# Spreading dependent chains over the pairs of a graph-attention kernel, and giving the first loads separate queues

## The chip, the cores and the metric

The kernel runs on one core of a Trainium2 chip. The metric is the time of one execution on the device in microseconds, as the median of several runs. The core has five engines with a queue of instructions each, which they work off in order: TensorE (PE, matmuls and transposes, results in PSUM), VectorE (DVE), ScalarE (ACT), GpSimd (POOL[...]) and SyncE (SP, which here only issues DMAs). DMAs are issued by SP, POOL and, with the change, ScalarE.

## The reference, cut to what matters

Four graph layers run one after the other on x (4096 x 256, float32), with one adjacency matrix adj (4096 x 4096, int32, about 32 neighbours in a row). Layers 0 and 2 hold an additive attention:

```python
h = relu(layernorm(x))
Wh = h @ W                                 # 4096 x 256
e = Wh @ a_src + (Wh @ a_dst).T            # 4096 x 4096
e = where(e > 0, e, slope * e)             # slope 0.2 in layer 0, 0.01 in layer 2
e = where(adj > 0, e, -9e15)               # -1e12 in layer 2
h_attn = softmax(e, axis=1) @ Wh
# layer 0: h_attn goes into a larger dense block, and x = x + block(...)
# layer 2: x = x + elu(h_attn)
```

Layer 1 is a mean over the neighbours, layer 3 an attention with dot products. The change does not touch their own code.

## The kernel before, in words

Rows are taken in tiles of 128 (NT = 32 tiles). The class Attention serves layers 0 and 2. It works in blocks of RB = 4 row tiles (layer 0 begins with two blocks of two), and within a block over the 32 column tiles in 16 pairs (PPB = 16). The loop of `run` has one turn for each pair n. A turn does these things in the source:

- `ahead(n)` (layer 0 only, its call is fresh): adjacency tiles are loaded by POOL's queue (adj_t, L486), transposed on TensorE into cT (L495) and turned by ScalarE into mask codes (turned, L500). FRESH says how many pairs this is ahead. In layer 2 the codes come back from DRAM instead (turned<-codesT on SP, L914).
- `reach(n + PPB + lead)` for a pair of the next block: VectorE keeps a running minimum of code minus destination score in PSUM (run, L278 and L280). LEAD says how many pairs this is ahead.
- `top(b)`, called in the turn in which a block's last minimum is issued: ScalarE copies run into SBUF (run_sb, L291), TensorE transposes it (top, L294), VectorE reduces and makes two rows of offsets from it (m and ab, L297 to L302), TensorE transposes these (abT, L304), ScalarE copies abT (L306), and it goes out to DRAM and back to all partitions as ab_row (SP, L319 and L320). Blocks 0 to 2 of layer 0 spread it by matmuls instead (L313, `spread` is 3).
- `logits` of pair n: VectorE makes y from ab_row and a PSUM copy b of it (L332; ScalarE makes b once a block, L330), and POOL subtracts the code (L336). There are eight buffers of y.
- Three pairs later (LAG): ScalarE's exponential of y (L363) and TensorE's 16 matmuls into four accumulators acc (L374; eight matmuls in a block of two). Column 0 of v is one, so that column 0 of acc is the sum of the row.
- At a block's last pair: VectorE takes the reciprocal of every sum (rden, L382), and `finish` scales the accumulators, half of them on VectorE and half on ScalarE: `finish0` writes xs (L447, L449), `finish2` writes hp (L926, L930), from which it makes exponential linear units and adds the rows of xs (L934 to L937). Layer 0 has four accumulators, layer 2 five.

PSUM tiles and y are released when their last reader is done. The order of the instructions on each engine is not just that of the source: when the program is built, a scheduler fills each engine's queue from the source's order and its own estimate of when operands are ready. On the chip that order is fixed.

Ahead of layer 0's run stands a preparation (`block0`): eight loads of x (xs, L610, on SP), with W and the two vectors a between the first and the second (L223 and L230, on SP too), then for each of eight blocks statistics, centring (L629, L633), transposes (L145), projections by W (L154) and minima.

## Time and profile before

| | |
|---|---|
| median of 3 runs | 2985.78 us (2985.42 to 2987.26) |
| the profiled execution, its own time | 2990.5 us |
| its span, first to last instruction | 2988.7 us |
| mean granted TensorE clock | 0.989 |
| TensorE busy (matmuls) | 2866.0 us |
| VectorE, ScalarE, POOL busy | 1907.1, 1279.1, 947.8 us |
| layer 0, preparation and attention | 0 to 626 us |
| layer 0, dense part | 626 to 1240 us |
| layer 1 | 1240 to 1500 us |
| layer 2, attention | 1531 to 2016 us |
| layer 3 | 2016 to 2989 us |

The profile comes from one execution. A group's line names the source line, the engine, the operation, the output and inputs by the program's names, shapes and count, then the busy time and the mean of one in ns, then the idle time of that engine just before these instructions and what ended it. In a list of waits a line reads "engine, waiting instruction <- engine, instruction it waited for: us in total, times, longest". A timeline's line has the start, the duration, the instruction, its count, and in brackets the idle time before it with what ended it.

### The profile page before, as it was taken

Reading aid. Unit: us, or ns where it says so; the run is one execution under the profiler, and the core shown is the slowest. Engines: PE = TensorE matmul, PEld = TensorE weight load, DVE = VectorE, ACT = ScalarE, POOL = GpSimd, SP = SyncE. Lnnn points to the kernel's source line nnn. Section 1 sums busy time; section 2 is a strip of 40 time slices with the busy share of each in tenths; the row PEclk is TensorE's granted clock in tenths of the full one; section 3 lists DMA queues with packets and bytes.
Section 4 is the critical chain, followed back from the end, with each engine's and each line's share of the span. In section 5 each row is a group of like instructions: output and inputs, shape, how many; then the busy total and the mean of one; then the engine's idle time right before and its main releaser. Section 6 shows DMA issues by size and latency. Waiting matters only on the chain.

```text
span 2988.7 us, 35212 instructions
## 1 busy us (share of the span) xinstructions
PE 2866.0 (96%) x13381; PEld 2335.5 (78%) x13381; DVE 1907.1 (64%) x3458; ACT 1279.1 (43%) x1963; POOL 947.8 (32%) x718
## 2 busy tenths in 40 slices
PE   7989999999999999899989999999999999999999
PEld 5778888866556665788878777888888888888888
DVE  5777777534555554477689888646766566566653
ACT  5666655459997323892264433433212112111211
POOL 4667665544444433220045555540000000000000
PEclk9999999999999999999999999999999999999999
DMA  5766665234553000595342122002111111111100
GB/s 131 201 146 145 128 139 133 71 58 70 80 79 65 8 8 8 136 248 164 113 170 87 68 78 78 29 11 68 58 51 47 37 34 62 39 34 62 34 8 8
DMA packets 109161, 238.62 MB, mean 80 GB/s; under 512 B 10736, under 2 KB 31200, under 8 KB 100288
## 3 DMA queue, kind: packets, MB, share of 16 engines
q1 hardware_dynamic: 71296, 167.26, 16.3%
q0 software_dynamic: 37696, 69.11, 14.9%
q8 instruction: 105, 1.72, 0.2%
q14 instruction: 64, 0.52, 0.1%
HBM read 265.63 MB, written 37.81 MB: 102 GB/s over the span
## 4 chain that ended last, share of the span: by engine, by line
PE 66%; ACT 9%; DVE 8%; issue 6%; POOL 6%; DMA 4%; SPq 0%; POOLq 0%; DVEq 0%; ACTq 0%
PE acc L374 18%; PE acc L1287 15%; PE s L154 15%; PE mm L154 8%; PE acc L1019 8%; POOL y L336 4%; ACT sign L180 4%; DVE y L332 2%; DVE run L280 2%; DMA turned<-codesT 1%; PE cT L495 1%; DMA a<-in_adj_dram 1%; PE q_ps L154 1%; ACT t L712 1%; DMA xs<-in_x_dram 1%
## 5 line engine op out<-in xcount | busy, mean ns | idle before, releaser
L374 PE MATMUL acc<-v,y 128*128 128x257 f32 x4096 | 930.8, 386 | 23.9 <-ACT hp L930 12.7
L374 PEld LDWEIGHTS acc<-v,y 128*128 128x128 f32 x4096 | 776.2, 192 | 137.0 <-ACT hp L930 17.0
L336 POOL TENSOR_TENSOR y<-y,turned 128x1024 f32<-128x1024 f32 (+1 forms) x272 | 545.3, 2015 | 320.2 <-DVE y L332 260.1
L363 ACT ACTIVATE y<-y,sdst 128x512 f32<-128x512 f32 (+1 forms) x544 | 350.5, 690 | 410.9 <-POOL y L336 410.7
L332 DVE SCALAR_TENSOR_TENSOR y<-ab_row,cdst,b 128x512 f32<-128x512 f32 (+1 forms) x544 | 371.0, 710 | 139.9 <-PE acc L374 124.1
L1287 PE MATMUL acc<-v,y 128*128 128x257 f32 x2048 | 454.5, 380 | 0.4 <-DVE rden L1295 0.4
L154 PE MATMUL s<-qT,hT 128*128 128x256 f32 x2048 | 445.2, 379 | 0.7 <-ACT qT L1235 0.7
L1280 ACT ACTIVATE y<-y 128x1024 f32<-128x1024 f32 x128 | 132.2, 1055 | 714.3 <-DVE y L1279 710.0
L154 PEld LDWEIGHTS s<-qT,hT 128*128 128x128 f32 x2048 | 389.0, 190 | 54.2 <-ACT qT L1235 1.4
L1287 PEld LDWEIGHTS acc<-v,y 128*128 128x128 f32 x2048 | 387.1, 190 | 55.9 <-issue 0.8
L180 ACT ACTIVATE sign<-a,limits 128x1024 bf16<-128x1024 bf16 x256 | 293.8, 1148 | 18.5 <-DMA a<-in_adj_dram 13.0
L1249 DVE SCALAR_TENSOR_TENSOR y<-code,s 128x512 f32<-128x512 bf16 x256 | 175.8, 687 | 100.7 <-PE s L154 100.5
L280 DVE SCALAR_TENSOR_TENSOR run<-turned,v,run 128x512 f32<-128x512 bf16 (+1 forms) x279 | 193.2, 692 | 31.8 <-ACT turned L500 22.7
L280 DVE SCALAR_TENSOR_TENSOR run<-turned,dst,run 128x512 f32<-128x512 bf16 x248 | 186.5, 752 | 24.5 <-DMA turned<-codesT 20.4
L1279 DVE TENSOR_TENSOR y<-y,top 128x1024 f32<-128x1024 f32 x128 | 146.2, 1215 | 43.0 <-PE top L1273 43.0
L1256 DVE TENSOR_TENSOR mx<-mx,y 128x512 f32<-128x512 f32 x224 | 154.8, 691 | 7.5
L500 ACT ACTIVATE turned<-cT,log_wide 128x1024 bf16<-128x1024 bf16 x128 | 139.2, 1105 | 29.9 <-PE cT L495 29.5
L173 POOL DMA_DIRECT2D a<-in_adj_dram x128 | 75.1, 588 | 198.4 <-ACT sign L180 144.8
L154 PE MATMUL mm<-kept 128*128 128x512 f32 x288 | 135.5, 610 | 2.4 <-ACT sz L807 1.4
L1019 PE MATMUL acc<-early,eq 128*128 128x512 f32 x512 | 128.8, 401 | 2.2 <-DVE early L421 1.9
L1019 PE MATMUL acc<-late,eq 128*128 128x512 f32 x512 | 122.6, 391 | 0.0
L1019 PEld LDWEIGHTS acc<-early,eq 128*128 128x128 f32 x512 | 97.0, 191 | 26.2 <-DVE early L421 2.1
(233 smaller groups left out, 3007.1 us busy)
## 6 DMA issues: line engine op xcount, KB each, us to landing
turned<-codesT SPq DMA_DIRECT2D x36, 1024.0 KB, 4.8
adj_t<-in_adj_dram POOLq DMA_DIRECT2D x128, 256.0 KB, 5.5
codesT<-turned SPq DMA_DIRECT2D x32, 1024.0 KB, 5.1
a<-in_adj_dram POOLq DMA_DIRECT2D x128, 256.0 KB, 4.7
code<-codesT SPq DMA_DIRECT2D x128, 256.0 KB, 5.5
code<-codesT SPq DMA_DIRECT2D x64, 512.0 KB, 8.1
ab_row<-l_ab_d SPq DMA_DIRECT2D x14, 512.0 KB, 5.6
xs<-in_x_dram SPq DMA_DIRECT2D x8, 512.0 KB, 12.5
```

The source lines that it names most:

```text
L154: nc.tensor.matmul(out=ps, lhsT=lhsT_of(k), rhs=rhs_of(k), start=(k == 0), stop=(k == n - 1))
L180: nc.scalar.activation(sign, self.came[g], AF.Sign, bias=limits[:, v : v + 1], accum_out=over[:, t, v, q : q + 1],)
L280: nc.vector.scalar_tensor_tensor(st["run"], code, dst, st["run"], ALU.subtract, ALU.min)
L332: nc.vector.scalar_tensor_tensor(y[:, :, k, :], st["ab"][:, 0, :, :], self.cdst[:, c + k : c + k + 1], st["b"], ALU.add, ALU.max,)
L336: nc.gpsimd.tensor_tensor(y, y, mask[:, :, c % QT : c % QT + 2, :], ALU.subtract)
L363: nc.scalar.activation(y[:, :, k, :], y[:, :, k, :], AF.Exp, bias=self.sdst[:, c + k : c + k + 1],)
L374: nc.tensor.matmul(out=acc, lhsT=y[:, r, k, :], rhs=self.v[:, c + k, 0 : D + 1], start=(c + k == 0), stop=(c + k == NT - 1),)
L1019: nc.tensor.matmul(out=acc, lhsT=eqs[c // (NT // 2)][:, ts(c % (NT // 2), P)], rhs=v1[c // BT][:, c % BT, :, :], start=(c == 0), stop=(c = ...
L1249: nc.vector.scalar_tensor_tensor(y[:, :, c : c + 2, :], st["code"][:, :, c : c + 2, :], -BIG / UNIT, ps, ALU.mult, ALU.add,)
L1256: nc.vector.tensor_tensor(mx, mx, y[:, :, c : c + 2, :], ALU.max)
L1279: nc.vector.tensor_tensor(part, part, top, ALU.subtract)
L1287: nc.tensor.matmul(out=accs[r], lhsT=st["y"][:, r, c, :], rhs=v3[:, c, :], start=(c == 0), stop=(c == NT - 1),)
```

## The change

What each part does:

- `top` becomes a generator with three pauses. It is put into a list `tasks`, and one link of each task is issued at the end of every turn of `run` (`step`): nothing in the turn of the last minimum, the transposes in the next turn, the reduction in the one after, abT and its way to ab_row in the third. Block 0's is issued at once (`drain`).
- The last minimum of a block writes straight into the SBUF tile run_sb, and ScalarE's copy of run falls away.
- At a block's end ScalarE copies every accumulator's 256 sums (raw) and its column 0 (den) out of PSUM. `finish` is a generator too: one reciprocal of den on VectorE a turn later, then the scaling, in place. In layer 0 VectorE scales. In layer 2 ScalarE scales, POOL takes a minimum, ScalarE the exponential, POOL adds the rows of xs (VectorE does both for the last block), and VectorE ends it, one link a turn.
- W and the two a are issued by ScalarE, so that SP has x alone. Two adjacency tiles instead of one are asked for ahead of the rest.
- LEAD goes from 5 to 6 and FRESH from 8 to 9.

```diff
+        def step(self):
+            for g in list(self.tasks):
+                if next(g, StopIteration) is StopIteration:
+                    self.tasks.remove(g)
+        def drain(self):
+            while self.tasks:
+                self.step()
...
+                to = st["run"]
+                if j == NT - 1:
+                    to = self.row_p.tile([P, RB, P], F32, tag="run", name="run_sb", bufs=1)
+                    to = to[:, 0:n, :]
                 if j == 0:
-                    nc.vector.tensor_scalar(st["run"], code, dst, None, ALU.subtract)
+                    nc.vector.tensor_scalar(to, code, dst, None, ALU.subtract)
                 else:
                     nc.vector.scalar_tensor_tensor(
-                        st["run"], code, dst, st["run"], ALU.subtract, ALU.min
-                    )
+                        to, code, dst, st["run"], ALU.subtract, ALU.min
+                    )
+                st["run"] = to
             if c == NT - 2 and not self.held:
-                self.top(b)
+                self.tasks.append(self.top(b))
+                if b == 0:
+                    self.drain()
         def top(self, b):
-            run = self.row_p.tile([P, RB, P], F32, tag="run", name="run_sb", bufs=1)[:, 0:n, :]
-            nc.scalar.copy(run, st["run"])
+            yield
             ps = self.ps_top.tile([P, RB, P], F32, tag="top", name="top")[:, 0:n, :]
             for r in range(n):
-                nc.tensor.transpose(ps[:, r, :], run[:, r, :], ident)
+                nc.tensor.transpose(ps[:, r, :], st["run"][:, r, :], ident)
+            yield
             src = self.v[:, at : at + n, D + 1]
...
             nc.vector.scalar_tensor_tensor(ab[:, 1, :], src, self.slope, m, ALU.mult, ALU.subtract)
+            yield
             ps = self.ps_top.tile([2 * n, P], F32, tag="top", name="abT")
...
                     if c == NT - 2:
                         done = accs.pop(b)
-                        rden = self.small.tile([P, RB], F32, tag="rden", name="rden")
+                        at, n_r = self.blocks[b]["at"], self.blocks[b]["n"]
+                        den = self.small.tile([P, n_r], F32, tag="den", name="den")
+                        raw = self.room(at, n_r)
                         for r, acc in enumerate(done):
-                            nc.vector.reciprocal(rden[:, r : r + 1], acc[:, 0:1])
-                        self.finish(self.blocks[b]["at"], done, rden)
+                            nc.scalar.copy(raw[:, r, :], acc[:, 1 : D + 1])
+                            nc.scalar.copy(den[:, r : r + 1], acc[:, 0:1])
+                        rden = self.small.tile([P, n_r], F32, tag="rden", name="rden")
+                        self.tasks.append(self.finish(at, raw, den, rden))
+                self.step()
+            self.drain()
...
-    LEAD = 5
+    LEAD = 6
     FIRST = 8
-    FRESH = 8
+    FRESH = 9
...
+            def room0(at, n):
+                return xs[:, at : at + n, :]
+            def finish0(at, raw, den, rden):
+                yield
+                nc.vector.reciprocal(rden, den)
+                for r in range(raw.shape[1]):
+                    nc.vector.tensor_scalar(
+                        raw[:, r, :], raw[:, r, :], rden[:, r : r + 1], None, ALU.mult
+                    )
...
-                load(1)
+                load(2)
+                att.weights(
+                    wp, w["L0_gnn_W"], (w["L0_gnn_a_src"], w["L0_gnn_a_dst"]), nc.scalar
+                )
                 for b in range(NB):
                     nc.sync.dma_start(
                         out=xs[:, ts(b, BT), :],
                         in_=x[ts(b, BW), :].rearrange("(t p) d -> p t d", p=P),
                     )
-                    if b == 0:
-                        att.weights(
-                            wp, w["L0_gnn_W"], (w["L0_gnn_a_src"], w["L0_gnn_a_dst"]), nc.sync
-                        )
...
+    def room2(at, n):
+        return work2.tile([P, RB, D], F32, tag="hp", name="hp")
+    def finish2(at, h, den, rden):
+        last = at == NT - RB
+        yield
+        nc.vector.reciprocal(rden, den)
+        yield
+        for r in range(RB):
+            nc.scalar.activation(
+                h[:, r, :], h[:, r, :], AF.Identity, scale=rden[:, r : r + 1], bias=minus
+            )
+        yield
         e = work2.tile([P, RB, D], F32, tag="e", name="e")
-        nc.scalar.activation(e, h, AF.Exp, bias=ones[:, 0:1])
+        (nc.vector if last else nc.gpsimd).tensor_scalar(e, h, -1.0, None, ALU.min)
+        yield
+        nc.scalar.activation(e, e, AF.Exp, bias=ones[:, 0:1])
+        yield
         rows = xs[:, at : at + RB, :]
-        nc.vector.scalar_tensor_tensor(e, e, 1.0, rows, ALU.min, ALU.add)
+        (nc.vector if last else nc.gpsimd).tensor_tensor(e, e, rows, ALU.add)
+        yield
         nc.vector.scalar_tensor_tensor(rows, h, -1.0, e, ALU.max, ALU.add)
```

More of the change, by code (lines that the diff above doesn't have):

```diff
@@ L192, with __init__ @@
     class Attention:
-        def __init__(self, es, tag, slope, lag, n_y, blocks, turned, finish, ps_top=None):
+        def __init__(self, es, tag, slope, lag, n_y, blocks, turned, room, finish, ps_top=None):
             self.tag, self.slope, self.lag, self.n_y = tag, slope, lag, n_y
-            self.turned, self.finish = turned, finish
+            self.turned, self.room, self.finish = turned, room, finish
+            self.tasks = []
             self.blocks = [{"at": at, "n": n} for at, n in blocks]
@@ L441 @@
         with ExitStack() as es:
-            def finish0(at, accs, rden):
-                for r, acc in enumerate(accs):
-                    dst, by = xs[:, at + r, :], rden[:, r : r + 1]
-                    if r % 2:
-                        nc.vector.tensor_scalar(dst, acc[:, 1 : D + 1], by, None, ALU.mult)
-                    else:
-                        nc.scalar.mul(dst, acc[:, 1 : D + 1], by)
+            def room0(at, n):
[7 more added lines that the diff above has]
+                    )
             turned = {}
@@ L460 @@
             ps_c = es.enter_context(tc.tile_pool(name="ps_c", bufs=2, space=PSUM))
-            att = Attention(es, "l0", 0.2, 3, 8, cuts, turned_of, finish0, ps_c)
+            att = Attention(es, "l0", 0.2, 3, 8, cuts, turned_of, room0, finish0, ps_c)
             att.hold(v0, "right")
@@ L918 @@
     nc.gpsimd.memset(minus, -1.0)
-    def finish2(at, accs, rden):
-        h = work2.tile([P, RB, D], F32, tag="hp", name="hp")
-        for r, acc in enumerate(accs):
-            by = rden[:, r : r + 1]
-            if r % 2:
-                nc.vector.tensor_scalar(
-                    h[:, r, :], acc[:, 1 : D + 1], by, -1.0, ALU.mult, ALU.add
-                )
-            else:
-                nc.scalar.activation(
-                    h[:, r, :], acc[:, 1 : D + 1], AF.Identity, scale=by, bias=minus
-                )
+    def room2(at, n):
[10 more added lines that the diff above has]
+        yield
         e = work2.tile([P, RB, D], F32, tag="e", name="e")
-        nc.scalar.activation(e, h, AF.Exp, bias=ones[:, 0:1])
+        (nc.vector if last else nc.gpsimd).tensor_scalar(e, h, -1.0, None, ALU.min)
+        yield
+        nc.scalar.activation(e, e, AF.Exp, bias=ones[:, 0:1])
+        yield
         rows = xs[:, at : at + RB, :]
-        nc.vector.scalar_tensor_tensor(e, e, 1.0, rows, ALU.min, ALU.add)
+        (nc.vector if last else nc.gpsimd).tensor_tensor(e, e, rows, ALU.add)
+        yield
         nc.vector.scalar_tensor_tensor(rows, h, -1.0, e, ALU.max, ALU.add)
     cuts2 = [(t, RB) for t in range(0, NT, RB)]
-    att2 = Attention(l2, "l2", 0.01, 3, 8, cuts2, None, finish2)
+    att2 = Attention(l2, "l2", 0.01, 3, 8, cuts2, None, room2, finish2)
     one2 = l2.enter_context(tc.tile_pool(name="l2_one", bufs=1))
@@ L1113 @@
                 pass
-            att2.top(0)
+            att2.tasks.append(att2.top(0))
+            att2.drain()
             run_staggered(blocks, 1)
```

## The prediction

> **What bounds the kernel now.** I read the page first, then the chain of waits, then the two attention stages (layer 0 up to 626 us, layer 2 from 1531 to 2016 us) in the timeline of TensorE, because the diff touches only those and the first 60 us.
>
> ```profile
> PE 2866.0 (96%) x13381; PEld 2335.5 (78%) x13381; DVE 1907.1 (64%) x3458; ACT 1279.1 (43%) x1963; POOL 947.8 (32%) x718
> ...
> L374 PE MATMUL acc<-v,y 128*128 128x257 f32 x4096 | 930.8, 386 | 23.9 <-ACT hp L930 12.7
> L374 PEld LDWEIGHTS acc<-v,y 128*128 128x128 f32 x4096 | 776.2, 192 | 137.0 <-ACT hp L930 17.0
> ```
>
> TensorE bounds the kernel. The matmuls into acc are the largest group, and 24 us of idle time stand just before them. A gain can only come from such idle time. The list of waits names what ends it:
>
> ```profile
> DVE rden L382 <- PE acc L374: 44.7, 20, 24.9
> ...
> ACT hp L930 <- DVE rden L382: 27.0, 8, 14.4
> ...
> PE abT L304 <- DVE ab L302: 22.1, 14, 3.0
> DVE m L297 <- PE top L294: 21.3, 5, 10.3
> ...
> PEld acc L374 <- ACT hp L930: 17.0, 10, 3.4
> ...
> PE acc L374 <- ACT hp L930: 12.7, 10, 3.0
> ```
>
> Two chains are seen. At each new maximum TensorE transposes (top), VectorE reduces (m, ab), and TensorE stands at abT until that is done: 22.1 us in 14 waits. At each block's end the accumulators come free through VectorE's reciprocal and then ScalarE (hp), and the next block's matmuls stand for them. Two layer-2 blocks in TensorE's timeline:
>
> ```profile
> 1682.16 0.27 PE L304 MATMUL abT<-ident,ab 128*8 128x128 f32 x1 [2.07 <-DVE ab L302]
> 1682.27 30.02 PE L374 MATMUL acc<-v,y 128*128 128x257 f32 x130
> 1713.38 0.70 PE L374 MATMUL acc<-v,y 128*128 128x257 f32 x2 [1.08 <-ACT hp L930]
> 1715.54 23.68 PE L374 MATMUL acc<-v,y 128*128 128x257 f32 x108 [1.46 <-ACT hp L930]
> ...
> 1745.30 27.90 PE L374 MATMUL acc<-v,y 128*128 128x257 f32 x128
> 1776.18 0.70 PE L374 MATMUL acc<-v,y 128*128 128x257 f32 x2 [2.99 <-ACT hp L930]
> 1778.35 25.36 PE L374 MATMUL acc<-v,y 128*128 128x257 f32 x108 [1.46 <-ACT hp L930]
> ```
>
> Undisturbed, a matmul costs 0.218 us (27.90 / 128). After the 2.99 us gap 108 of them take 25.36 us, 0.235 each: a gap is followed by slow matmuls, here 1.8 us more.
>
> **Size of the prize.** Layer 2: the last block, which has neither maximum nor successor, takes 56.2 us (1959.9 to 2016.1); with 0.6 us for the four transposes and abT, 56.85. The seven before it take 429.0 us (1530.9 to 1959.9), against 398: **31 us** lost (idle 13.1 before abT, 14.6 before acc, the rest slow matmuls). Layer 0 from 170.9 to 569.8: five blocks of 16 pairs at 3.97 us plus 0.6 (64.1 each) and one of about 58.8, since no adjacency is left to transpose after 526 us; 379 against 399: **19.5 us** lost (7.8 before abT, 9.3 before acc, one slow stretch at 508 us). Before 171 us TensorE idles 14.1 us up to 76 and 12.1 after (its gaps in the timeline added up).
>
> **What the Trainium skill says.** "ScalarE: Activation LUTs", section What ACT_TABLE_LOAD costs: an ACTIVATE with immediate scale and bias takes 186 ns + 0.833 ns per element, and back-to-back ones overlap by about 93 ns. The trace agrees roughly: the 256-wide copy lo<-acc takes 372 ns (399 by the page). "SBUF — State Buffer", section Who interferes with whom: a VectorE instruction with two SBUF inputs, or a tensor_scalar in a 2-port mode, shares a port with GpSimd under an exclusive lock. The trace agrees: L298, 4 elements wide, takes 1.30 us in layer 0 and 0.16 us unhindered, and L936 takes 2.30 us where L937 of the same size takes 1.21. "TensorE: Matmul & The Clock Gate", section What's actually happening: idling lowers the clock to half; the stretch from 165 to 170 us shows a granted clock of 0.50. "DMA: Bandwidth & Descriptors", section Issuing engines are not separate DMA queues: more issuing engines save issue time alone. The first 35 us agree, with the DMA share at 1.1 whatever the issuer.
>
> **The change, part by part.**
>
> *1. Links of the maximum.* Removed: run_sb's copy on ScalarE (17 x 0.57 us, beside other work) and with it VectorE's wait for it in run L278 (7 us in layer 2). Moved: the transposes come one pair after the last minimum, the reduction a pair later, abT a pair later again. LEAD 6 starts it one pair earlier, so abT stands two pairs later than before. Between top and abT TensorE now has a pair, 3.5 to 3.97 us, against VectorE's chain of 2.8 us (0.68+0.30+1.02+0.63+0.15, layer-2 means). I take 0.3 us left per block of 1.1 to 3.0: gain 20.9 less 4, **17 us** (10 to 20). VectorE still stops at m until TensorE reaches top, with more logits done by then; behind it are run and the y logits, and GpSimd and ScalarE wait for those. y has 8 buffers, and "DVE y waits for PE acc" (45.7 us in layer 2) shows VectorE at the end of them, so this is covered. If the cover were gone, it costs the m wait, up to 10.3 us once.
>
> *2. Later ab_row.* On SP the store of abT and the load of ab_row move two pairs later, past one turned load or codesT store at times. From abT to the copy b took 1562.33 to 1569.05, 6.7 us; then 1.4 (two logits), 2.1 (POOL), 1.3 (exponentials): 12 us. abT came 28 to 31 us ahead of the border; two pairs later leaves 21 to 24. Cost nothing, 9 us of cover.
>
> *3. Block ends.* Per block ScalarE does four 256-wide copies and four 1-wide ones instead of two scalings, and VectorE's reciprocals (4 x 0.16) and two scalings (0.48) go off the path. A 1-wide copy is in no trace: from 0.09 us (overlapped) to 0.25 (abT_sb, 128 wide); I take 0.187, the page's. With overlaps a row takes 0.37 us, four rows 1.5; the first row is complete 0.66 us before the last, so the last is free about 0.9 us after the final matmul, and the next block wants it 0.66 us after (later with layer 0's transposes of 0.45 us; layer 2 has a fifth accumulator). An exponential (0.71) or a turned (1.1) in between adds to that: 0.7 us left per border. Gain: 14.6 + 9.3 idle and 6 of slow matmuls (31 + 19.5 less all four idle sums), 30, less 13 x 0.7: **21 us** (5 to 27). Behind a copy that waits for TensorE stand exponentials; some seven pairs of y are done ahead, which covers them.
>
> *4. Finishing.* Layer 0: four tensor_scalars SBUF to SBUF, 0.31 us alone (L633), up to 2.4 behind a POOL subtraction; I take 0.8, so VectorE goes from 1.6 to 3.4 us a block, in a slack of 16 (2.98 of every 3.97 us used). Layer 2: VectorE loses L936 (2.3), L926 (1.0) and three reciprocals (0.5). ScalarE gains four in-place scalings (2.2) and loses two. POOL gains a tensor_scalar, 2.3 us (from L810, 1.56 for half the width, and L633), and an addition (2.36, L846), 4.7 a block where it is busy 34 of 57. Each can hold the y behind it for 2.3 us: covered by the pairs ahead. Nothing taken; 0 to -8 us. The last block's chain is 4 us longer after 2016 us, beside layer 3's preparation, whose last block starts some 30 us later: nothing.
>
> *5. Start.* SP's W and two a issues (0.50+0.46+0.43) go to ScalarE, idle until 4.8 us, so x1 is issued at 1.2 instead of 2.75 us; a second adjacency load on POOL (0.57 us, past the cast of identb, not needed before 13 us) competes. The bytes stay, and transfers are saturated to 35 us: the last awaited x (33.5 us) hardly moves. Taken: 2 us (-1 to +4).
>
> *6. LEAD and FRESH.* One more pair of minima before the run (2 x 0.48 us on VectorE, idle 3.6 us between 65 and 70); no further transposes ahead of it: needed(24) is 12 units, as needed(23) is. Buffers still come free four pairs ahead. With it VectorE's stops at m (4.2 us at 99, 10.3 at 149), in a stretch where it is 100% busy otherwise, shrink by the logits and minima that go ahead: 4 us of the 12 idle (0 to 10).
>
> Sum: 17 + 21 + 2 + 4 = 44 us, of which I take 38, because each engine's order is fixed at build by an estimate (in this trace top at 149 us stands behind several pairs that come after it in the source). The profiled execution took 2990.5 us (span 2988.7), 0.16% over the median of 2985.78; 38 us off the median is 2948.
>
> **Rivals.**
>
> *A. Borders stay.* ScalarE, alone with 1.5 us of copies and exponentials between, frees accumulators no sooner than two engines did (0.3 to 3 us), while the 17 us of part 1 come, and little at the start: 2966 (2956 to 2979). For it: layer 0's border at 304.3, where an exponential stood ahead of xs. Against: ScalarE is busy 192 of 473 us in layer 2. Chance 0.21.
>
> *B. Slower: ab_row too late.* If the build puts abT more than 9 us, 2.6 pairs, behind the source's place, ab_row lands after the stored y are used up, and each further pair costs 3.5 us in seven borders of layer 2 and 3.97 in the six of layer 0 that go by DMA (spread is 3): 48 us. One pair past the point outweighs the 38 us and gives 2996. For it: SP puts a turned load between store and load (at 1686.3), and "ACT b waits for DMA ab_row" already is 21 us. Against: the cover above. Chance 0.12.
>
> *C. The order is the same in effect.* The build already moves instructions to where it thinks them ready, and issues the links where they stood: 2985. Against: run_sb and the reciprocals are off the path whatever the order. Chance 0.05.
>
> **Numbers.** Forecast 0.62 at 2948 us (2924 to 2960). A measurement can tell 0.2%, 6 us. Faster by more: forecast and A, 0.83; within: C, 0.05; slower: B, 0.12. The range runs from 2924 (both gains whole and more of the front) to 2979 (A's end).
>
> **What would show it.** Right: "PE abT waits for DVE ab" falls from 22 us to under 5; "PE acc waits for ACT hp" is gone and under 10 us stand before acc, ended by the copies raw; layer-2 blocks of 57 to 59 us. For A: abT's wait gone, but 20 us before acc. For B: ACT b's wait for ab_row at 30 us and more, with gaps after each block's first logits. Part 5 is wrong if the last projection ends before 58 us or after 63. I am wrong altogether if TensorE's idle time in 1531 to 2016 us stays at 28 us, or if GpSimd's y becomes what it waits for.

## The result, and the profile after

| | before | changed |
|---|---|---|
| median of four runs | 2986.11 us (2985.42 to 2987.26) | 3019.64 us (3016.88 to 3023.41) |
| ratio to before | | 1.0113 (95% interval 1.0095 to 1.0130) |
| profiled execution, own time | 2990.5 us | 3021.13 us |
| its span | 2988.7 us | 3019.4 us |
| mean granted TensorE clock | 0.989 | 0.982 |

The change makes the kernel 33 us slower, where the prediction had 38 us faster. The same lines of the page as before, engines and then the matmuls into acc (busy time in us, mean of one in ns, then idle time just before them and what ended most of it):

```profile
PE 2882.4 (95%) x13381; PEld 2346.2 (78%) x13381; DVE 1898.2 (63%) x3405; ACT 1294.3 (43%) x2074; POOL 981.0 (32%) x732
...
L393 PE MATMUL acc<-v,y 128*128 128x257 f32 x4096 | 949.8, 390 | 60.5 <-ACT den L405 33.6
```

The idle time ahead of acc has grown from 23.9 to 60.5 us, and the same 4096 matmuls are busy 19 us longer. By the profile 33.6 us of it are ended by the copy den, the last instruction that ScalarE does on an accumulator. Most of the rest lies in layer 0 and is put down to "issue", but there too the matmuls start as a den ends (at the border of 303.06 us, shown in the last section, ScalarE has this before it):

```profile
302.80 0.16 ACT L405 COPY den<-acc 128x1 f32<-128x1 f32 x1
```

The list of waits of layer 2's stage (1560 to 2033 us; total, times, longest) says the same, and shows what became of the other wait:

```profile
ACT y L382 <- POOL y L355: 209.1, 116, 6.3
...
ACT b L349 <- DMA ab_row<-l_ab_d: 46.5, 7, 7.2
...
PE acc L393 <- ACT den L405: 31.2, 13, 5.1
...
PE abT L323 <- DVE ab L320: 4.3, 4, 2.2
```

The wait for ab before abT is down to 4.3 us, as wanted. The wait for the accumulators, 12.7 us before, is 31.2. And ScalarE's wait for ab_row at b has grown to 46.5 us from that of the kernel before (same window):

```profile
ACT b L330 <- DMA ab_row<-l_ab_d: 18.9, 4, 4.8
```

Where the 30.7 us between the two spans lie, by stage (ends of the stages read from the first and last matmul into acc), with TensorE's idle time in the two attention stages (here and below without the 1.9 to 2.0 us before layer 2's very first matmul into acc, the same in every run):

| stage, us | before | changed | difference | idle before acc | idle before abT |
|---|---|---|---|---|---|
| start to first acc | 76.3 | 76.1 | -0.2 | | |
| to the first block of four | 94.6 | 83.9 | -10.7 | | |
| rest of layer 0's attention | 455.6 | 475.1 | +19.5 | 9.3 to 24.3 | 7.8 to 0 |
| dense part and layer 1 | 904.4 | 905.9 | +1.5 | | |
| layer 2's attention | 485.2 | 503.2 | +18.0 | 12.7 to 31.2 | 13.1 to 4.3 |
| layer 3 | 972.6 | 975.3 | +2.7 | | |

Idle time explains about half of the two losses: 15.0 less 7.8 us in layer 0, 18.5 less 8.8 in layer 2. Most of the rest is slow matmuls (the last section shows what makes them slow). The view by windows gives the busy time of each engine and the granted clock (PEclk); first before:

```profile
171.00:626.00 455.00, 437.84 (x2471) 377.30 (x2470) 301.62 (x474) 243.29 (x335) 280.92 (x192) 0.99 0.52 117
...
1531.00:2016.00 485.00, 459.27 (x2084) 395.72 (x2085) 368.56 (x588) 197.31 (x306) 273.75 (x134) 0.98 0.17 62
```

and of the changed kernel:

```profile
160.00:635.00 475.00, 448.40 (x2490) 385.51 (x2489) 305.93 (x468) 247.37 (x377) 281.33 (x194) 0.96 0.49 112
...
1541.00:2044.00 503.00, 467.56 (x2084) 400.91 (x2085) 353.00 (x542) 211.21 (x374) 308.18 (x148) 0.96 0.17 60
```

The second number is TensorE's busy time: in layer 2 the same 2084 instructions take 8.3 us more, at a clock of 0.96 instead of 0.98.

One border of layer 2 in TensorE's timeline, from an abT to the next:

```profile
1640.64 21.40 PE L393 MATMUL acc<-v,y 128*128 128x257 f32 x98
1666.21 0.70 PE L393 MATMUL acc<-v,y 128*128 128x257 f32 x2 [4.17 <-ACT den L405]
1667.68 30.12 PE L393 MATMUL acc<-v,y 128*128 128x257 f32 x124 [0.77 <-ACT den L405]
1697.64 0.60 PE L311 MATMUL top<-ident,run_sb 128*128 128x128 f32 x4
1698.08 7.10 PE L393 MATMUL acc<-v,y 128*128 128x257 f32 x32
1705.44 0.27 PE L323 MATMUL abT<-ident,ab 128*8 128x128 f32 x1 [0.26 <-DVE ab L320]
```

The 98 matmuls after abT run at 0.218 us each. Then TensorE stands 4.17 and 0.77 us, and the next 124 take 0.243 each on average, 3.1 us more than at 0.218. A block takes 65 us where 57 to 59 were expected. Now ScalarE at the same border:

```profile
1640.84 0.26 ACT L325 COPY abT_sb<-abT 8x128 f32<-8x128 f32 x1 [0.59 <-PE abT L323]
1647.18 0.59 ACT L349 COPY b<-ab_row 128x512 f32<-128x512 f32 x1 [6.08 <-DMA ab_row<-l_ab_d]
1654.05 1.34 ACT L382 ACTIVATE y<-y,sdst 128x512 f32<-128x512 f32 x2 [6.29 <-POOL y L355]
1656.15 1.33 ACT L382 ACTIVATE y<-y,sdst 128x512 f32<-128x512 f32 x2 [0.76 <-POOL y L355]
1658.24 1.33 ACT L382 ACTIVATE y<-y,sdst 128x512 f32<-128x512 f32 x2 [0.76 <-POOL y L355]
1660.34 1.33 ACT L382 ACTIVATE y<-y,sdst 128x512 f32<-128x512 f32 x2 [0.76 <-POOL y L355]
1662.43 1.33 ACT L382 ACTIVATE y<-y,sdst 128x512 f32<-128x512 f32 x2 [0.76 <-POOL y L355]
1664.51 1.33 ACT L382 ACTIVATE y<-y,sdst 128x512 f32<-128x512 f32 x2 [0.74 <-POOL y L355]
1665.75 0.35 ACT L404 COPY hp<-acc 128x256 f32<-128x256 f32 x1
1666.00 0.16 ACT L405 COPY den<-acc 128x1 f32<-128x1 f32 x1
```

This view holds the answer. The new block starts on TensorE at 1661.45 and wants its first used accumulator at 1662.04. The two copies that free it are 0.51 us of work, but on ScalarE's queue **twelve exponentials (six pairs) of the new block** stand ahead of it. Each pair waits for GpSimd, which needs 2.1 us for one. The sixth is done at 1665.84, and the copies start with it. In the kernel before the sixth pair is done in time (ScalarE's timeline at the border of 1711.9 us):

```profile
1708.77 1.33 ACT L363 ACTIVATE y<-y,sdst 128x512 f32<-128x512 f32 x2 [1.35 <-POOL y L336]
1712.76 0.56 ACT L930 ACTIVATE hp<-acc,minus,rden 128x256 f32<-128x256 f32 x1 [2.66 <-DVE rden L382]
```

The pair at 1708.77 is the sixth. ScalarE then stands free for 2.66 us and waits for VectorE's reciprocal. In layer 2 twelve exponentials stand ahead of ScalarE's first instruction on the old block's accumulators at every border of both kernels but one (thirteen, in the kernel before); only the time at which they can run has moved. Relative to the border, that is the end of the block before's last matmul (layer 2, the five borders in the middle; ends of abT and of the exponentials, starts of the logits):

| us from the border | before | changed |
|---|---|---|
| abT | -29.4 to -27.3 | -20.8 |
| first logits on VectorE | -20.4 to -16.9 | -11.4 to -10.7 |
| sixth pair's exponential done | -1.8 to -1.3 | +4.2 to +4.9 |

### The profile page after: what moved, and what is told of

The parts are those of the page before. It is cut to its first block, busy times and chain, and to the rows that moved or that the text cites. A ratio compares the mean times of both kernels' runs of the same rounds, so it can differ in the third digit from the quotient of the medians.

```text
span 3019.4 us, 35240 instructions
## 1 busy us (share of the span) xinstructions
PE 2882.4 (95%) x13381; PEld 2346.2 (78%) x13381; DVE 1898.2 (63%) x3405; ACT 1294.3 (43%) x2074; POOL 981.0 (32%) x732
## 3 DMA queue, kind: packets, MB, share of 16 engines
q0 software_dynamic: 37696, 69.11, 14.9%
## 4 chain that ended last, share of the span: by engine, by line
PE 63%; DVE 9%; issue 8%; ACT 8%; POOL 7%; DMA 6%; SPq 0%; POOLq 0%; DVEq 0%; ACTq 0%
PE acc L393 17%; PE acc L1320 15%; PE s L154 15%; PE mm L154 8%; PE acc L1051 4%; ACT sign L180 4%; POOL y L355 3%; DVE run L295 3%; DVE y L351 3%; DMA a<-in_adj_dram 2%; DMA turned<-codesT 1%; PE tp L723 1%; PE cT L524 1%; PE q_ps L154 1%; DMA xs<-in_x_dram 1%
## 5 line engine op out<-in xcount | busy, mean ns | idle before, releaser
L393 PE MATMUL acc<-v,y 128*128 128x257 f32 x4096 | 949.8, 390 | 60.5 <-ACT den L405 33.6
L1320 PE MATMUL acc<-v,y 128*128 128x257 f32 x2048 | 454.5, 380 | 0.4 <-DVE rden L1328 0.4
L295 DVE SCALAR_TENSOR_TENSOR run<-turned,v,run 128x512 f32<-128x512 bf16 (+1 forms) x270 | 186.6, 691 | 67.2 <-ACT turned L529 59.1
L529 ACT ACTIVATE turned<-cT,log_wide 128x1024 bf16<-128x1024 bf16 x128 | 139.9, 1103 | 33.5 <-PE cT L524 33.2
L173 POOL DMA_DIRECT2D a<-in_adj_dram x128 | 76.1, 595 | 199.0 <-ACT sign L180 144.4
L154 PE MATMUL mm<-kept,zT 128*128 128x256 f32 x512 | 114.7, 380 | 0.5 <-ACT zT L750 0.5
```

Of the source, the lines that this page charges most:

```text
L154: nc.tensor.matmul(out=ps, lhsT=lhsT_of(k), rhs=rhs_of(k), start=(k == 0), stop=(k == n - 1))
L295: nc.vector.scalar_tensor_tensor(to, code, dst, st["run"], ALU.subtract, ALU.min)
L393: nc.tensor.matmul(out=acc, lhsT=y[:, r, k, :], rhs=self.v[:, c + k, 0 : D + 1], start=(c + k == 0), stop=(c + k == NT - 1),)
L1320: nc.tensor.matmul(out=accs[r], lhsT=st["y"][:, r, c, :], rhs=v3[:, c, :], start=(c == 0), stop=(c == NT - 1),)
```

## The experiments

The theory after the comparison is the one above, in two steps: the links put ab_row later, and six pairs of exponentials then hold back the copies. The rivals: the new copies on ScalarE are too slow in themselves; GpSimd's two new instructions of a block (2.77 and 2.35 us) push y; lateness alone, whatever stands in ScalarE's queue. Every experiment but before_again changes the changed kernel; ratios are to the kernel before on the same chip.

| run | median us, ratio (95%) | layer 0 rest, us: idle before acc, abT | layer 2, us: idle before acc, abT | to first block of four |
|---|---|---|---|---|
| changed | 3019.64, 1.0113 | 475.1: 24.3, 0 | 503.2: 31.2, 4.3 | 83.9 |
| e1_top_at_once | 3007.18, 1.0049 (1.0030 to 1.0068) | 463.0: 7.0, 11.1 | 493.7: 6.4, 23.5 | 96.9 |
| e2_lead8_l2 | 3001.17, 1.0032 (1.0021 to 1.0044) | 474.2: 23.5, 0 | 487.2: 23.3, 2.9 | 81.9 |
| e3_old_finish | 3004.45, 1.0043 (1.0032 to 1.0054) | 481.9: 28.1, 0 | 487.6: 25.7, 0 | 81.3 |
| e4_lead5 | 2998.05, 1.0022 (1.0013 to 1.0031) | 471.5: 23.1, 0 | 492.3: 28.7, 0 | 79.6 |
| e5_six_y | 3002.18, 1.0035 (1.0022 to 1.0048) | 491.6: 30.9, 0 | 483.9: 21.2, 0.6 | 86.1 |
| e6_five_y | 2995.15, 1.0015 (1.0000 to 1.0030) | 482.3: 28.6, 0 | 486.3: 21.5, 5.8 | 81.7 |
| e7_spread_all | 3015.94, 1.0077 (1.0057 to 1.0097) | 480.1: 5.3, 0 | 502.0: 31.1, 4.8 | 81.8 |
| e8_lead8_pool | 3002.78, 1.0037 (1.0025 to 1.0049) | 474.7: 23.3, 0 | 488.2: 21.6, 5.3 | 83.7 |
| e9_copies_first | 2983.67, 0.9987 (0.9977 to 0.9998) | 461.4: 0, 0 | 484.2: 0, 25.3 | 84.2 |
| e10_copies_first_lead5 | 2944.81, 0.9861 (0.9845 to 0.9876) | 445.9: 0, 0 | 464.9: 1.0, 11.3 | 79.6 |
| e11_at_once_copies | 2982.09, 0.9972 (0.9964 to 0.9979) | 446.4: 0, 8.4 | 496.6: 0, 38.0 | 83.0 |

**e1_top_at_once.** The links are issued at once, in the turn of the last minimum:

```diff
-                self.tasks.append(self.top(b))
-                if b == 0:
-                    self.drain()
+                for _ in self.top(b):
+                    pass
```

> The changed kernel, but the whole chain of a maximum is issued in the turn of the last minimum, as before the change; the finish, LEAD 6 and FRESH 9 stay changed. Late-row theory (abT and ab_row come later, so the next block's first logits are late, and the copies of the accumulators stand on ScalarE behind exponentials that wait for them): TensorE's idle time before acc in layer 2 falls from 31 us to 15 or less, abT's waits return (13 us in layer 2, 8 in layer 0), total 2970 to 2990 us. Copy theory (ScalarE alone, with eight copies, frees the accumulators later than two engines did): the 31 us before acc stay, abT's waits come on top, total 3020 or more. GpSimd theory (the minimum and the addition on GpSimd hold up y): as the copy theory, 3015 or more.

The waits of TensorE in layer 2 (1554 to 2050 us):

```profile
PE abT L322 <- DVE ab L319: 23.5, 7, 4.4
PE acc L392 <- ACT den L404: 6.4, 6, 1.5
```

With abT 32 to 34 us ahead of the middle borders, the sixth pair's exponentials end 1.8 us before them, and the wait for the accumulators is 6.4 instead of 31.2 us, with the same copies on ScalarE. So the copies are not what is slow. The time gained goes back into the wait before abT, and the 11 us of the front are gone again (96.9 us). So the total is a miss: 3007.18 us, still above the kernel before.

**e2_lead8_l2.** Layer 2 issues its minima two pairs earlier, so that row and links come earlier too:

```diff
-            for n in range(PPB, PPB + LEAD):
+            for n in range(PPB, PPB + 8):
...
-        att2.run(es, LEAD, 5)
+        att2.run(es, 8, 5)
```

> The changed kernel with layer 2's LEAD at 8 instead of 6, layer 0 as it is: abT comes two pairs (7 us) earlier in every block of layer 2. Late-row theory: layer 2 from first to last matmul falls from 503 us to 470 to 482, total 2987 to 2998. Copy theory and GpSimd theory: 503 us stay, total 3016 to 3023.

Layer 2 is 16 us shorter, not the 21 to 33 expected, and the sixth pair's exponentials end at the border (-1.1 to +1.7 us). But 23.3 us of acc waits stay: copies three and four now stand behind one of the seventh pair's two exponentials, whose y is late too. Moving the row by two pairs mends one queue position, not the rule.

**e3_old_finish.** The kernel before's block ends (VectorE's reciprocals, two scalings on each engine, no work of GpSimd) with the spread links:

```diff
-                            nc.scalar.copy(raw[:, r, :], acc[:, 1 : D + 1])
-                            nc.scalar.copy(den[:, r : r + 1], acc[:, 0:1])
-                        rden = self.small.tile([P, n_r], F32, tag="rden", name="rden")
-                        self.tasks.append(self.finish(at, raw, den, rden))
+                            nc.vector.reciprocal(rden[:, r : r + 1], acc[:, 0:1])
+                        self.finish(self.blocks[b]["at"], done, rden)
```

> The changed kernel with the finish of before (VectorE's reciprocals straight from the accumulators, scaling half on VectorE and half on ScalarE, no work on GpSimd, nothing spread over turns); the links of the maxima stay one beside each pair. Late-row theory: the borders stay as bad, 25 us or more before acc in layer 2, total 3005 or more. Copy theory: the gaps before acc fall to 13 us in layer 2 and 9 in layer 0 as before the change while abT's waits stay gone, total 2960 to 2972. GpSimd theory: the same, 2960 to 2975.

TensorE's waits in layer 0 (150 to 640 us):

```profile
PE acc L393 <- ACT xs L471: 26.8, 6, 5.4
```

TensorE stands about as long with the old block ends, 28.1 and 25.7 us, so neither the copies nor GpSimd's two instructions are needed for these waits. That isn't to say that the new ends are free: layer 2 is 15.6 us shorter here than in the changed kernel (5.5 of it before acc, 4.3 before abT, the rest in TensorE's busy time), and layer 0 is 6.8 us longer. Which of the two new things does that was not tried.

**e4_lead5.** LEAD back to 5, all else as changed.

```diff
-    LEAD = 6
+    LEAD = 5
```

> The changed kernel with LEAD 5 instead of 6 in both layers: abT comes one pair later. Late-row theory: every border of layer 2 loses up to a pair more (3.5 us) and those of layer 0 some too, total 3030 to 3060. Copy theory and GpSimd theory: within 5 us of 3020.

This is a miss. I expected it to be much slower, since the row comes a pair later still (abT 17.3 us ahead of the border in layer 2). It is faster than the changed kernel. Its gaps before acc are of the same size (28.7 us in layer 2), since ScalarE has ten or eleven exponentials ahead of the first copy instead of twelve, and the waits before abT are gone. Lateness alone does not set the gap; which exponentials stand in the queue counts with it.

**e5_six_y and e6_five_y.** Fewer buffers of y, so that fewer pairs can be ahead (e6 has 5 in place of 6 here):

```diff
-            att = Attention(es, "l0", 0.2, 3, 8, cuts, turned_of, room0, finish0, ps_c)
+            att = Attention(es, "l0", 0.2, 3, 6, cuts, turned_of, room0, finish0, ps_c)
...
-    att2 = Attention(l2, "l2", 0.01, 3, 8, cuts2, None, room2, finish2)
+    att2 = Attention(l2, "l2", 0.01, 3, 6, cuts2, None, room2, finish2)
```

> The changed kernel with six buffers of y instead of eight in both layers. Queue theory (12 exponentials of the next block, six pairs, stand on ScalarE ahead of the first copy of an accumulator; with abT late they are done only 2 to 5 us after the block's last matmul, so the copies and TensorE wait): fewer buffers let fewer exponentials go ahead, four pairs instead of six, which are done 4.2 us sooner, so the idle time before acc falls from 24 us in layer 0 and 31 in layer 2 to 12 or less each, total ratio 0.990 to 1.003 against before. Plain lateness (what counts is that TensorE runs out of y after a border): two buffers less make it worse, ratio 1.012 or more.

> The changed kernel with five buffers of y. Queue theory: three pairs ahead of the copies, no wait for them any more, under 6 us before acc at the borders; but only five pairs are ahead of TensorE in the steady part, so that VectorE's waits for y's buffers grow and some gaps may come from late exponentials: ratio 0.988 to 1.005. Plain lateness: ratio 1.015 or more.

Mostly a miss. In layer 2 the wait falls from 31.2 to about 21 us with eight and six exponentials ahead, where 12 or less and under 6 were expected. In layer 0 it grows. At e6's borders of layer 0 only six exponentials are ahead, but ScalarE's masks and signs of 1.1 us each stand between them and the copies. In layer 2 the third pair itself is late; ScalarE at the border of 1830.3 us in e6:

```profile
1832.38 1.33 ACT L382 ACTIVATE y<-y,sdst 128x512 f32<-128x512 f32 x2 [5.53 <-POOL y L355]
...
1833.62 0.35 ACT L404 COPY hp<-acc 128x256 f32<-128x256 f32 x1
```

Its y waited for VectorE, which had stood 4.08 us for a turned from DRAM. So it isn't the count as such: the copy comes after the *latest* exponential that is queued ahead of it, and a smaller count only helps where the last one comes earlier. In these two kernels the dense part and layer 1 are also some 20 us shorter (886.6 and 883.1 us) and the start some 10 us longer than in the others. Why was not tried.

**e7_spread_all.** All blocks of layer 0 spread the row by matmuls, none by DRAM:

```diff
-            att.picks, att.spread = picks.tile([n, n, P], F32, name="picks"), 3
+            att.picks, att.spread = picks.tile([n, n, P], F32, name="picks"), len(cuts)
```

> The changed kernel with all of layer 0's rows spread by matmuls on TensorE instead of by DMA (spread 9 instead of 3); layer 2 as it is. Queue theory: b is there 5 to 6 us sooner after abT, so the six pairs of exponentials are done before the border, and layer 0's idle time before acc falls from 24 us to 12 or less, while TensorE spends 2 us more in each of six blocks: layer 0 from the first four-row block to its end 460 to 472 us against 475. If the DMAs' way plays no part: 480 us or more.

TensorE's waits in layer 0 (150 to 640 us):

```profile
PE spread L332 <- ACT abT_sb L325: 10.5, 5, 3.8
PE acc L393 <- issue: 4.3, 5, 2.0
PE acc L393 <- ACT den L405: 1.0, 1, 1.0
```

The mechanism is as expected: the logits start 19 to 23 us ahead of the borders, the sixth pair is done by then, and the acc wait falls from 24.3 to 5.3 us, in layer 0 alone. The stage's length is a miss: 480.1 us against the 460 to 472 that I expected. The spreading matmuls wait for ScalarE's abT_sb (10.5 us), and TensorE is busy 464.2 us in the stage instead of 448.5.

**e8_lead8_pool.** e2, with layer 2's turned loads on GpSimd's queue instead of SP's:

```diff
-            nc.sync.dma_start(out=loaded[b, q], in_=codesT[b][q])
+            nc.gpsimd.dma_start(out=loaded[b, q], in_=codesT[b][q])
```

> The changed kernel with LEAD 8 in layer 2 and layer 2's loads of codes (turned) on GpSimd's queue instead of SP's, so that abT's store and load are not queued behind a turned load that waits for its buffer. Queue theory: b comes 7 to 9 us after abT instead of 13, its six pairs of exponentials end 3 us or more before the border, and layer 2's idle time before acc is under 9 us (23 with LEAD 8 alone): layer 2 from first to last matmul 466 to 476 us. If SP's queue is not what delays b: 487 us as with LEAD 8 alone.

No different from e2 within the intervals. The row does come earlier: the first logits start 17.5 to 18.0 us ahead of four middle borders, where e2 has 13.9 to 14.6. But copies three and four still stand behind an exponential of the seventh pair, and 21.6 us of waits stay. A row that is 3 us earlier was not enough.

**e9_copies_first.** The decisive one for the waits. Nothing is issued earlier; the exponentials of a block's third pair and later (c is the pair's first column tile) come after the last copy of the block before in ScalarE's queue. This is an order only, no wait:

```diff
-                    for k in range(2):
-                        nc.scalar.activation(
-                            y[:, :, k, :], y[:, :, k, :], AF.Exp,
-                            bias=self.sdst[:, c + k : c + k + 1],
-                        )
+                    with tc.issue_after(copied) if copied and c >= 4 else ExitStack():
+                        for k in range(2):
+                            nc.scalar.activation(...)
...
-                            nc.scalar.copy(den[:, r : r + 1], acc[:, 0:1])
+                            copied = nc.scalar.copy(den[:, r : r + 1], acc[:, 0:1]).ins
```

> The changed kernel with one edit of order alone: the exponentials of a block from its third pair on are queued on ScalarE behind the copies of the block before, so that four exponentials (two pairs) instead of twelve stand ahead of the copies. abT and ab_row stay as late as they are. Queue theory: the waits for the copies go, idle time before acc falls from 24 + 31 us to 15 or less in all, and with it the slow matmuls after each gap; layer 2 from 503 to 462 to 474 us, layer 0 from the first four-row block on from 475 to 446 to 458, ratio against before 0.983 to 0.993. If the late rows starve TensorE whatever the order (its y are not ready after the border): gaps move behind the first two pairs and the ratio stays at 1.005 or more.

The waits for the copies are gone in both layers, though the first logits come only 12.4 to 13.4 us ahead of the middle borders in layer 2; e2, with 13.9 to 18.8 us, kept 23.3 us of those waits. That confirms the queue and refutes lateness as such. The total is a miss: 0.9987, above the 0.983 to 0.993 that I expected, with both layers longer than expected. The longest of TensorE's waits are now these (layer 2, 1540 to 2028 us, then layer 0, 150 to 640 us):

```profile
PE abT L323 <- DVE ab L320: 25.3, 5, 5.7
```

```profile
PE cT L525 <- ACT turned L530: 19.6, 16, 2.2
```

The time shows up before abT (VectorE now has ab 11 to 12.5 us after top) and before the transposes of the adjacency.

**e10_copies_first_lead5.** e9 with LEAD 5 (both edits above).

> The same with LEAD 5 instead of 6: rows a pair later. Queue theory: two pairs of exponentials are still done some 3 us before the border, so within 8 us of the same kernel with LEAD 6, ratio 0.982 to 0.994. If the lateness itself counts: 1.002 or more, and clearly slower than with LEAD 6.

2944.81 us, ratio 0.9861 (0.9845 to 0.9876): faster than both kernels. The ratio is in the expected range, but I expected it within 8 us of e9, and it is 38.9 us below; no theory had that. A line of its page, and its waits of TensorE in layer 2 (1520 to 1990 us):

```profile
L394 PE MATMUL acc<-v,y 128*128 128x257 f32 x4096 | 921.0, 383 | 3.9 <-ACT y L383 2.0
```

```profile
PE abT L323 <- DVE ab L320: 11.3, 5, 2.9
...
PE acc L394 <- ACT y L383: 1.0, 2, 0.5
```

The idle time before acc is 3.9 us in all, and the 4096 matmuls are busy 921.0 us, 28.8 fewer than in the changed kernel. ScalarE at the border of 1732.7 us:

```profile
1729.89 1.33 ACT L383 ACTIVATE y<-y,sdst 128x512 f32<-128x512 f32 x2 [0.77 <-POOL y L355]
1731.40 0.37 ACT L405 COPY hp<-acc 128x256 f32<-128x256 f32 x1 [0.17 <-PE acc L394]
1731.67 0.17 ACT L406 COPY den<-acc 128x1 f32<-128x1 f32 x1
...
1732.97 0.17 ACT L406 COPY den<-acc 128x1 f32<-128x1 f32 x1
1733.02 0.73 ACT L383 ACTIVATE y<-y,sdst 128x512 f32<-128x512 f32 x1
```

After two pairs the first copy waits for TensorE's last matmul on its accumulator (0.17 us), and the four rows are out in 1.74 us, at TensorE's pace of two matmuls a row, ahead of everything else. abT comes 17.3 to 19.0 us ahead of the border here and the first logits 8.7 to 10.5, later than in the changed kernel (20.8 and 10.7 to 11.4): it is the place in the queue that counts.

**before_again.** The kernel before itself, with a profile on the chip of e9 and e10.

> The kernel before, for its profile on this chip: stages and waits as in its first profile; the first matmul into acc shows whether the 5 us between 76 us (profiles of before and after) and 71 us (the experiments) are the chip's: then about 71 us here, and part 5 of the prediction (the loads' queues) brought nothing; if 76 us, the loads' queues brought 5 us.

2989.29 us; stages 75.3, 95.5, 457.3, 903.2 and 483.5 us. So e10's gain against it lies in the front (15.9 us), layer 0 (11.4) and layer 2 (18.6), and 3.2 us in the start. By the expectation 75.3 us speaks for the loads' queues; but kernels with the same loads differ by more than that from one profile to another (e1 to e4 have 70.7 to 72.7 us, the changed kernel 76.1), so it stays unclear.

**e11_at_once_copies.** e10 with e1's edit: what are the spread links worth once nothing holds back the copies?

> e10 (copies ahead of the fifth and later exponential, LEAD 5) with the links of the maximum issued at once, as the kernel before did. It asks what the spreading of the links is worth once the copies are no longer held back. My theory: the spreading is worth what part 1 of the prediction took from the waits before abT (about 17 us) plus what it gave in the front (11 us between the kernel before and the changed one), less the later row, which costs nothing where the copies go first. So TensorE should stand 8 to 13 us before abT in layer 0 and 12 to 24 in layer 2 (11.1 and 23.5 in e1), 0 to 3 before acc, the stretch from the first accumulation to the first block of four should take 90 to 97 us (79.6 in e10), and the time against the kernel before be 0.992 to 1.000. Rival: the spreading is worth nothing and all of e10's gain comes from the copies going first: then 0.983 to 0.989, with the stretch at the front near 80 and under 10 us before abT in each layer.

2982.09 us, ratio 0.9972 where e10 has 0.9861. Neither theory is right in its parts. In layer 2 (1520 to 2020 us):

```profile
PE abT L322 <- DVE ab L319: 38.0, 6, 8.4
```

There the spread links are worth 31.7 us (496.6 against 464.9), more than I expected. In layer 0 they are worth nothing (446.4 against 445.9), since 8.4 us before abT stand against e10's 10.3 before the adjacency's transposes. In the front it is 3.4 us (83.0 against 79.6), not ten.

## Why the prediction was wrong

**The step that failed is part 2**, "Cost nothing, 9 us of cover", together with part 3's "some seven pairs of y are done ahead, which covers them". Part 2 counted 12 us from abT to the *first* pair's exponentials and set it against the 21 to 24 us that are left, and part 3 had the exponentials behind the copy. What had to be done in time was the *sixth* pair, since six pairs are queued ahead of the copies. Five more pairs at GpSimd's 2.13 us add 10.7, so 22.7 us were needed, and 20.8 were there in layer 2. Measured at the border shown above: first pair 14.9 us after abT (1640.53 to 1655.39; VectorE came to the first y 2.5 us late, behind eight minima), sixth pair 25.3 us. With 0.4 us for the copies that is 4.2 us after 1662.04, when the accumulator was wanted: the gap. Thirteen borders, with gaps of 0.6 to 6.3 us, make the 55.5 us of acc waits, 33.5 more than before, and the slow matmuls behind them add some 19 (10.6 and 8.3 in the view by windows).

The view that could have told it was the count: twelve exponentials stand ahead of ScalarE's first scaling in the kernel before as well, and the sixth pair's end lies only 1.3 to 1.8 us before the border there. GpSimd's line ahead of the border of 1772.8 us:

```profile
1757.44 12.60 POOL L336 TENSOR_TENSOR y<-y,turned 128x1024 f32<-128x1024 f32 x6 [8.78 <-DVE y L332]
```

It makes the six pairs without a break from the first, so the sixth ends as late as the row makes it: the true cover was under 2 us there, not 9. The 12 us were also read at the first border alone; at four of layer 2's seven, abT to the first pair's exponentials took 15.8 to 16.4 us. (The sixth pair's end alone doesn't tell this. In e1 it lies 1.8 us before the border too, with abT 32 us ahead and more: VectorE stands there for a buffer of y that TensorE has yet to free, 2.06 us at 1777.59.) I read the wait list, where "ACT hp waits for DVE rden", and took the queue ahead of it for free.

The queue is about half of the miss: e9, which mends nothing else, goes from 1.0113 to 0.9987, some 38 us, and the forecast of 2948 us would be 0.987. The other half shows as the waits that e9 has before abT and before the adjacency's transposes, with slow matmuls after them, and it is gone with LEAD 5 in place of 6 (e10). So part 6's longer lead, counted as a gain, failed as well; why it costs that much stays open.

Point by point:

- *Part 1 (17 us)* had the right wait and too large a gain. abT's 20.9 us of idle time became 4.3, but in a kernel in which TensorE stood before acc instead. Where the copies are free, layer 0 has none left, while layer 2 has 11.3 us in e10 and 25.3 in e9 (13.1 before), and waits before the adjacency's transposes are new. That the links are worth spreading shows in e11 against e10.
- *Part 3 (21 us)* had the copies' own size right: a 256-wide one takes mostly 0.35 to 0.38 us and a sum 0.16 to 0.18 (0.187 was taken), four rows back to back 1.42 us in e1 (1.5 was taken). With 0 and 1.0 us before acc in e10, the 22.0 us of idle time there are nearly all gained. (The prediction has 23.9; 1.9 of them stand before layer 2's first matmul in every run and were not to be had.)
- *Part 4* (0 to -8) is near in its prices and unsettled as a whole: with the old finish e3 has about the same waits, but a shorter layer 2 and a longer layer 0. Layer 0's scalings take 0.86 us each (0.8 was taken), GpSimd's two 2.77 and 2.35 (2.3 and 2.36).
- *Part 5* (2 us): in the first two profiles the last projection ends at 62.3 us instead of 62.4; on one other chip the start is about 3 us shorter. Unclear. The DMA share that this part leans on is 1.10 to 1.12 only from 10 to 35 us, with SP and POOL both issuing; in the first 10 us it is 0.56 and 0.98.
- *Part 6* (4 us of the front) was too small there: the front gained 10.7. But it is not LEAD that gave it: e4 and e10, with LEAD 5, have 79.6 us, and e1, with LEAD 6 and the links at once, has 96.9. LEAD 6 costs time in the whole kernel: 38.9 us between e9 and e10.
- *Rival A* came nearest. Its sign came true and more (abT's wait nearly gone, 60.5 us before acc), and it named exponentials between the copies and a border where one stood ahead. It took the borders to stay as they were, though, and not to get worse, and laid it on ScalarE being alone: e3 has the waits with two engines, and e9 and e10 are rid of them with ScalarE alone.
- *Rival B* had the right place, a late ab_row, and the sign it named came true (46.5 us at b, over 30). Its point was wrong: it began only when abT lay 2.6 pairs behind its place in the source and y ran out. The loss began with abT at the very place that the prediction assumed, 20.8 to 26.0 us ahead, and it went by ScalarE's queue, while GpSimd was already at the seventh pair of y.
- *The sum* of 38 us was within 6 of what e10 brings against its kernel before (43.5 us). That is partly chance, since e10's gain is spread otherwise (more in the front, less at the borders).

What stays open: why the order with LEAD 6 is so much worse than with LEAD 5, also in the front, and the shift between start and dense part in e5 and e6. Of VectorE's 11 to 12.5 us from top to ab in e9, 7 to 8 pass before it comes to m, and 4.4 from m to ab with logits and a minimum in between; in e10 the second part is mostly 1.4 us with nothing in between. Every edit lets the build order all queues anew, so the totals carry more than the one change that an experiment is named for; the waits at the borders are the surer reading.

## What to carry to other kernels

When a chain is moved later, don't stop at its first consumer: find the last instruction that is fed by it and stands, in an engine's queue, ahead of something that releases a resource, and count the producer's pace for all of those. An instruction whose operands are ready is not free while its queue has late work ahead of it; short releasing instructions belong ahead of long-waiting ones, by order if not by time. And read the slack at the place itself (here the sixth pair's end against the border, and what holds that end), not from a list of waits, which names the last of several.

## What the runs showed of the hardware

After a gap of a few us TensorE runs at half its clock for a while, which costs time on top of the gap. The view by windows at the border shown above, ahead of the gap, just after it, and later (the second number is TensorE's busy time, with its matmuls in brackets; 0.50 and 1.00 are the granted clock):

```profile
1642.00:1661.00 19.00, 19.00 (x89) 16.66 (x88) 16.84 (x24) 5.25 (x9) 9.11 (x5) 1.00 0.13 52
1668.00:1673.00 5.00, 5.00 (x13) 3.89 (x13) 3.09 (x6) 4.20 (x9) 3.69 (x2) 0.50 0.08 16
1674.00:1697.00 23.00, 23.00 (x108) 20.14 (x107) 19.40 (x26) 8.97 (x13) 15.21 (x8) 1.00 0.19 75
```

By their starts in the trace, a matmul takes 0.43 us in the middle window and 0.22 in the others (the counts take in those that a window's ends cut). So the 0.243 us of the 124 matmuls are an average of some 14 slow ones and 110 at full speed, and the prediction's 0.235 after a gap of 2.99 us is one too. In layer 0 the same happens:

```profile
303.06 6.44 PE L393 MATMUL acc<-v,y 128*128 128x257 f32 x16 [3.72 <-issue]
```

The granted clock is 0.50 from 303 to 308 us; sixteen in undisturbed stretches of e6's layer 0 take 3.69 us. In the traces of the kernel before and the changed one, each stretch of half clock that begins in these stages lasts 3.41, 6.83 or 10.24 us. They cover 23.7 us of layer 0's rest and layer 2 in the kernel before, 71.6 us in the changed one and 6.8 us in e10. In all fourteen profiles every gap of more than 2.5 us before a matmul of these stages has one beside it (during the gap or beginning within 4 us of its end); of the shorter ones some have (2.07 us at 1682.16 in the kernel before) and some have not (2.21 us at 1771 in the changed one). That is why a stage with 7 us more idle time before acc and abT got 19.5 us longer.

ScalarE's copy of one element in each partition costs 0.16 to 0.22 us (median 0.17), close to half of one that is 256 wide (0.35 to 0.43, median 0.37).
